# A fused two-layer network on one core: other rounds for the projections and the turns of tokens of the next image

## The chip, the cores and the metric

The kernel runs on one core of one Trainium2 chip. The metric is the device time of one execution in microseconds (us), the median of several executions. The engines are named as the profile names them: PE (TensorE, matmuls; PEld its weight loads), DVE (VectorE), ACT (ScalarE), POOL (GpSimd) and SP (SyncE, which issues DMAs). PE writes its results into PSUM, a small memory of eight banks per partition, from which ACT and DVE read.

## What is computed

Two layers on an input of 8 images of 128 channels and 32 x 32 pixels. The change lies in the first step of layer 0, attention along the rows of an image. Cut to what matters:

```python
def _L0_conv_ref(x, wq, wk, wv):
    xp = jnp.transpose(x, (0, 2, 3, 1))
    q = (xp @ wq.T).reshape(b, h, w, n, d)      # n = 8 heads, d = 16
    k = (xp @ wk.T).reshape(b, h, w, n, d)
    v = (xp @ wv.T).reshape(b, h, w, n, d)
    weights = jnp.einsum('bhwnd,bxynd->bnhwxy', q, k) * scale
    weights = jax.nn.softmax(weights, axis=-1)   # over y alone
    attn = jnp.einsum('bnhwxy,bxynd->bhwnd', weights, v)
    return jnp.transpose(attn.reshape(b, h, w, c), (0, 3, 1, 2))
...
x = x + _L0_conv_ref(_ln_c(x), L0_conv_wq, L0_conv_wk, L0_conv_wv)
t = t + _L0_ffn_ref(_ln_t(t), ...)      # a spectral filter of the tokens
x = x + _L1_conv_ref(_ln_c(x), ...)     # a deformable convolution
t = t + _L1_ffn_ref(_ln_t(t), ...)      # a mixture of eight experts
```

Every one of the 1024 tokens of an image looks at all 1024, but the softmax is taken over each group of 32 tokens by itself. `_ln_c` normalises each pixel over its channels.

## The kernel before

Attention comes first and takes about a third of the span; the other three steps follow, and the change does not touch them. The inputs of this case take the function `attention_bounded`. It works in *rounds*. An image has 8 units (4 quarters of 256 queries, `qc`, times 2 groups of 4 heads, `hg`), and a unit has 4 rounds, so an image has 32 rounds and the whole 256. Image b starts at round `first = 32 * b`. In the text, "round 20" means round 20 of the 32 of whichever image is running, and "-8" means `first - 8`, which is round 24 of the image before.

The function writes a list `work` of pieces, each with a round and an order within the round, sorts it, and issues it in that order; no scheduler changes it afterwards. Each engine runs its own instructions in this order and waits in it. For a unit that starts in round t0 the pieces are:

- order 0, round t0 + r: `scores`, 8 matmuls on PE into the PSUM tile `s` (four banks, one buffer; L609), then the exponential of all of it on ACT (L614), into `e`.
- order 1, the same round: `add_tiles` on POOL (L623).
- order 2, rounds t0 + 8 to t0 + 11: `values` on PE (L661), 8 calls a round in the first, third and fourth, with 4 more of the next piece at order 6.5 in the first and the last 4 of it in the second.
- order 2.5, round t0 + 6: `spread_out` on PE (L644).
- order 3, rounds t0 + 6 to t0 + 9: `divide` on DVE (L651).
- orders 4 and 5, round t0 + 5: `sums` on PE (L630, 16 matmul calls), then `reciprocals` on DVE (L637).
- for every second unit, order 5, round t0 + 11: `take` on ACT (L671); order 6, round t0 + 12: `results`, 2 matmuls `po` on PE (L678), a copy `at<-po` on ACT (L682), an addition on POOL (L686), and after the last quarter the DMA of the image to `x1d` (L688). `results` thus always falls on a round that is 0 mod 8.

As every t0 is a multiple of 4, a round's work depends on its number mod 4: sums are in 1 mod 4, `spread_out` in 2 mod 4, one and a half pieces of `values` in 0 mod 4, and 3 mod 4 has only scores and one piece of `values` on PE. (The profile counts each fp32 matmul call as two instructions.)

Between these lie the preparations of the next image:

- `load` (order 6): one DMA on SP's queue into `xc`.
- `tokens` (order 5.5), twice: four transposes on PE (`pt`, L544) and a copy on ACT (`xt<-pt`, L546). `xt` has three buffers.
- the layer norm in 25 small pieces (order 6): 8 of statistics on DVE (L77, L78), 9 on POOL, 8 on ACT (L103), which write `ht`.
- `channels` (order 5.5), twice: four transposes on PE (`pb`, L552) and a copy on ACT (`hk<-pb`, L555).
- ten projections (order 6): `keys` (L578, copy L583), `queries` (L564, L569) and `key_values` (L590, L596), each one or four matmuls on PE with 512 columns in all and a copy of 512 columns on ACT.

`po`, `pt`, `pb`, `pk`, `pq`, `pv` and the sums `z` all come from `small_bank` (L532), one PSUM bank under the tag "z", in a pool with one buffer (L521). A piece that takes it waits until the reader of the piece before has read it. Pieces with the same round and order go in the order in which they were put on the list, the images one after the other, so `results` of an earlier image or quarter that fall into the same round as a projection of the next image stand before it. `project_at`, `turn` and `norm_at` (L710 to L722) hold the rounds of the preparations.

Of the kernel before, what the change touches and what calls it, by code (L numbers as in the profile page):

```python
# [63 lines left out]
def layer_norm_pieces(nc, pool, src, dst, eps):  # L64

    t = {}

    def stats(i):  # L70
        if i == 0:
            for name, shape in (
                ("st", [P, NT, 6]), ("mv", [P, NT, 2]), ("v", [P, NT]), ("y", [P, NT]),
                ("w", [P, NT]), ("nm", [P, NT]),
            ):
                t[name] = pool.tile(shape, F32, tag=f"lp_{name}", name=f"lp_{name}")
        nc.vector.bn_stats(t["st"][:, i, :], src()[:, i, :])  # L77
        nc.vector.bn_aggr(t["mv"][:, i, :], t["st"][:, i, :])  # L78

    def inverse(n):  # L80

        v, y, w, mv = t["v"], t["y"], t["w"], t["mv"]
        bits = [i.bitcast(I32) for i in (y, v)]
        ops = [
            lambda: nc.gpsimd.tensor_scalar(v, mv[:, :, 1], eps, None, ALU.add),
            lambda: nc.gpsimd.tensor_scalar(bits[0], bits[1], -0.5, 0x5F3759DF, ALU.mult, ALU.add),
            lambda: nc.gpsimd.tensor_scalar(v, v, -0.5, None, ALU.mult),
        ]
        ops += 3 * [
            lambda: nc.gpsimd.tensor_mul(w, y, y),  # L90
            lambda: nc.gpsimd.tensor_mul(w, w, v),
            lambda: nc.gpsimd.tensor_scalar(w, w, 1.5, None, ALU.add),
            lambda: nc.gpsimd.tensor_mul(y, y, w),
        ]
        ops += [
            lambda: nc.gpsimd.tensor_mul(t["nm"], mv[:, :, 0], y),
            lambda: nc.gpsimd.tensor_scalar(t["nm"], t["nm"], -1.0, None, ALU.mult),
        ]
        for op in ops[2 * n : 2 * n + 2]:
            op()  # L100

    def norm(i):
        nc.scalar.activation(  # L103
            dst()[:, i, :], src()[:, i, :], AF.Identity, bias=t["nm"][:, i : i + 1],
            scale=t["y"][:, i : i + 1],
        )

    return (
        [partial(stats, i) for i in range(NT)] + [partial(inverse, n) for n in range(9)]
        + [partial(norm, i) for i in range(NT)]  # L110
    )
# [388 lines left out]
def attention_bounded(ctx, tc, ident, x, x1d, given, weigh, begin_group):  # L500
# [192 lines left out]
    def at(round_no, order, do, *args):  # L693
        work.append((round_no, order, len(work), do, args))

    def spread_rounds(pieces, rounds):
        for piece, round_no in zip(pieces, rounds):
            at(round_no, 6, piece)

    for b in range(B):  # L700
        img = {}
        first = 4 * UNITS * b
        project = [
            (keys, img, 0, 0), (keys, img, 0, 1), (queries, img, 0, 0),
            (keys, img, 1, 0), (keys, img, 1, 1), (queries, img, 1, 0),
            (key_values, b, img, 0), (key_values, b, img, 1),
            (queries, img, 0, 1), (queries, img, 1, 1),
        ]
        if b == 0:
            turn = {"tokens": (0, 0)}  # L710
            project_at = (-1, -1, -1, 0, 1, 2, 3, 4, 7, 11)
        else:
            project_at = [first + n for n in (-13, -12, -9, -5, -4, -1, 3, 4, 7, 11)]
            turn = {"channels": (first - 20, first - 17)}
            if b == 1:
                turn.update(load=0, tokens=(2, 3))
                norm_at = (3, 3, 4, 4, 5, 5, 6, 6) + (6, 7, 7, 8, 8, 8, 9, 9, 9) + (
                    10, 10, 10, 11, 13, 13, 14, 14)
            else:
                turn.update(load=first - 42, tokens=(first - 38, first - 34))  # L720
                norm_at = [first - n for n in (
                    37, 36, 35, 34, 33, 32, 32, 31, *range(31, 22, -1), 22, 22, 22, 21, 19, 19, 18, 18  # L722
                )]
        if b:
            at(turn["load"], 6, load, b)
            spread_rounds(
                layer_norm_pieces(nc, sb, lambda i=img: i["xt"], lambda: given.ht, 1e-6), norm_at
            )
            for par in range(2):
                at(turn["channels"][par], 5.5, channels, par)  # L730
        for par in range(2):
            at(turn["tokens"][par], 5.5, tokens, img, par)
        for n, (step, when) in enumerate(zip(project, project_at)):
            if b == 0 and n < 3:
                at(-1, 6, weigh[n])
            at(when, 6, *step)
        for qc in range(QC):
            qrt = {}
            for hg in range(HG):
                un = {"at": (qc, hg)}  # L740
                t0 = first + 4 * (HG * qc + hg)
                for r in range(4):
                    at(t0 + r, 0, scores, img, un, r)
                    at(t0 + r, 1, add_tiles, un, r)
                    at(t0 + 5, 4, sums, un, r)
                    at(t0 + 6 + r, 3, divide, un, r)
                at(t0 + 8, 2, values, img, un, 0, (0, 1), qrt)
                at(t0 + 8, 6.5, values, img, un, 1, (0,), qrt)
                at(t0 + 9, 2, values, img, un, 1, (1,), qrt)
                at(t0 + 10, 2, values, img, un, 2, (0, 1), qrt)  # L750
                at(t0 + 11, 2, values, img, un, 3, (0, 1), qrt)
                at(t0 + 5, 5, reciprocals, un)
                at(t0 + 6, 2.5, spread_out, un)
            at(t0 + 11, 5, take, qrt)
            at(t0 + 12, 6, results, b, img, qc, qrt)
# [889 lines left out]
def metaformer_kernel(  # L1645
# [27 lines left out]
    with tc.If(bounded > P - 1) as branch:  # L1673
        with ExitStack() as part:
            attention_bounded(part, tc, ident, x, x1d, given, weigh, begin.pieces)
# [63 lines left out]
```

## Time and profile before

| | |
|---|---|
| median of 3 runs | 2681.59 us (2681.54 to 2681.8) |
| profiled execution, its time | 2682.64 us |
| its span, first to last instruction | 2680.9 us |
| first to last exponential of attention | 30.1 to 889.3 us |
| PE busy in the span | 2518.2 us (94%) |
| DVE, POOL, ACT busy in the span | 1857.6, 1448.4, 1074.7 us |
| granted TensorE clock, mean of the span; of 100 to 850 us | 0.972; 1.00 |
| one exponential (L614) | 1879 ns, x256 |
| one divide (L651), one addition (L623) | 2278 ns, 2376 ns, x256 each |
| copies on ACT of 512 columns (L546, L555, L569, L583, L596) | median 586 to 603 ns |
| copies on ACT of 256 columns (L671, L682) | median 365, 366 ns |

A line of a group reads: source line, engine, operation, tiles written and read, shapes, count, then busy time and mean time of one, then the idle time of the engine just before it and what ended that idle time. Modelled ends of pipelined matmuls overlap a little, so a group that follows another on PE starts some 0.07 us before the other's shown end. A line of the timeline reads: start, duration, engine, source line, operation, tiles, shapes, count, and in brackets the engine's idle time before it with what ended it.

### The profile page before, as it was taken

The page shows a single profiled execution, that of the slowest core. Times are in us where ns is not written, and L with a number is a line of the kernel's source. Part 1 is how long each engine was busy: PE and PEld are TensorE (multiplying, and loading weights), DVE is VectorE, ACT ScalarE, POOL GpSimd, SP SyncE. Part 2 cuts the span into 40 slices and gives each one's busy share as a digit, 9 for nine tenths or more (in the row PEclk, how much of TensorE's full clock was granted, in tenths as well). Part 3 has the DMA queues.
Part 4 walks back from the last instruction along what each step waited for, and adds up shares of the span by engine and source line. Part 5 has one row for each costly group of instructions (what it writes and reads, how often), then busy time and mean ns, then how long its engine had stood idle before and what let it go on. Part 6 is the DMA issues. An engine that isn't in the chain of part 4 may idle for free. (4 is left out here: it accounts for less than half of the span.)

```text
span 2680.9 us, 47231 instructions
## 1 busy us (share of the span) xinstructions
PE 2518.2 (94%) x18768; PEld 1758.2 (66%) x18768; DVE 1857.6 (69%) x2744; ACT 1074.7 (40%) x2014; POOL 1448.4 (54%) x1535
## 2 busy tenths in 40 slices
PE   6999999999999799999999999999999999999914
PEld 3555555555555478787777778778778778778712
DVE  3788888888888545548748738748748657758646
ACT  4676766766667211123223224214224224224222
POOL 4777777777788455446246236236237327226230
PEclk9999999999999899999999999999999999999956
DMA  1000000000000254475266265256266256246151
GB/s 29 2 17 2 17 17 2 17 2 18 10 18 17 63 172 150 133 209 177 71 203 189 72 196 176 89 179 194 79 185 187 92 161 209 87 138 217 46 171 34
DMA packets 213379, 271.29 MB, mean 101 GB/s; under 512 B 20820, under 2 KB 146964, under 8 KB 213152
## 3 DMA queue, kind: packets, MB, share of 16 engines
q1 hardware_dynamic: 190016, 209.46, 26.1%
q0 software_dynamic: 16800, 55.59, 6.3%
q10 hardware_dynamic: 6336, 3.15, 0.4%
q8 instruction: 150, 2.46, 0.4%
q14 instruction: 77, 0.63, 0.1%
HBM read 200.22 MB, written 67.92 MB: 100 GB/s over the span
## 5 line engine op out<-in xcount | busy, mean ns | idle before, releaser
L623 POOL TENSOR_TENSOR t<-e 128x1024 f32<-128x1024 f32 x256 | 608.2, 2376 | 200.9 <-ACT e L614 200.6
L651 DVE TENSOR_TENSOR e<-e,rb 128x2048 f32<-128x2048 f32 x256 | 570.8, 2278 | 83.6 <-PE rb L644 83.6
L614 ACT ACTIVATE e<-s 128x2048 f32<-128x2048 f32 x256 | 481.1, 1879 | 253.8 <-PE s L609 251.8
L1508 POOL TENSOR_TENSOR part<-us,part 128x256 f32<-128x256 f32 x256 | 189.8, 742 | 695.5 <-ACT part L1507 694.9
L1460 PE MATMUL po<-us,mf 128*128 128x128 f32 (+2 forms) x2048 | 529.0, 381 | 4.4 <-DVE mf L1392 4.4
L1513 DVE TENSOR_TENSOR part<-p_y,part 128x512 f32<-128x512 f32 x256 | 175.5, 686 | 303.7 <-PE p_y L1495 177.0
L1506 ACT COPY us<-p_x 128x256 f32<-128x256 f32 x256 | 95.0, 371 | 724.2 <-PE p_x L1495 721.9
L1460 PEld LDWEIGHTS po<-us,mf 128*128 128x128 f32 x2048 | 309.2, 191 | 36.4 <-DVE mf L1392 4.8
L609 PE MATMUL s<-q,k 32*128 32x256 f32 x4096 | 296.9, 404 | 14.3 <-ACT e L614 13.5
L661 PE MATMUL av<-e,vt 128*32 128x256 f32 x4096 | 288.7, 389 | 4.4 <-DVE e L651 3.1
L1523 DVE TENSOR_TENSOR us<-p_z,part 128x512 f32<-128x512 f32 x256 | 174.9, 683 | 150.7 <-PE p_z L1495 150.6
L609 PEld LDWEIGHTS s<-q,k 32*128 32x128 f32 x4096 | 186.7, 186 | 137.3 <-ACT e L614 116.0
L1495 PEld LDWEIGHTS p_z<-diff,gap 128*128 128x128 f32 x1024 | 192.2, 190 | 128.0 <-issue 87.9
L1495 PE MATMUL p_z<-diff,gap 128*128 128x256 f32 x1024 | 264.8, 380 | 3.5 <-DVE base L906 3.1
L1107 ACT ACTIVATE g<-g,w 128x128 f32<-128x128 f32 x512 | 161.4, 394 | 112.2 <-DMA g<-tab,here 90.8
L1089 POOL DMA_INDIRECT g<-tab,here x168 | 166.0, 988 | 69.7 <-issue 30.5
L661 PEld LDWEIGHTS av<-e,vt 128*32 128x32 f32 x4096 | 101.4, 109 | 141.8 <-issue 84.5
L1115 DVE TENSOR_REDUCE x<-g 128x128 f32<-128x1536 f32 x64 | 180.4, 2818 | 6.8 <-ACT g L1107 1.2
L1250 POOL TENSOR_TENSOR diff<-teto 128x516 f32<-128x516 f32 x127 | 163.9, 1291 | 1.3 <-DMA teto<-in_phi_o 0.5
L637 DVE RECIPROCAL r<-z 128x256 f32<-128x256 f32 x64 | 112.5, 1758 | 70.8 <-PE z L630 70.6
L1495 PE MATMUL p_y<-diff,gap 128*128 128x256 f32 x512 | 152.9, 380 | 0.1
L1495 PE MATMUL p_z<-teto,ht 128*128 128x256 f32 x512 | 133.0, 382 | 0.0
(262 smaller groups left out, 3702.6 us busy)
## 6 DMA issues: line engine op xcount, KB each, us to landing
mf<-mfd SPq DMA_DIRECT2D x112, 512.0 KB
tab<-gs SPq DMA_DIRECT2D x180, 256.0 KB
teto<-in_phi_o SPq DMA_DIRECT2D x127, 256.5 KB
teto<-in_phi_e SPq DMA_DIRECT2D x127, 256.0 KB
mfd<-mf SPq DMA_DIRECT2D x16, 512.0 KB
xc<-in_x SPq DMA_DIRECT2D x8, 512.0 KB
x1d<-xt SPq DMA_DIRECT2D x8, 512.0 KB
m_room<-in_M_plus SPq DMA_DIRECT2D x16, 256.0 KB
```

The source lines that it names most:

```text
L609: nc.tensor.matmul(s[:, j, c, :], img["k"][rows, hg, 2 * r + c, :], q[rows, qc * QU : (qc + 1) * QU], start=True, stop=True,)
L614: nc.scalar.activation(e.rearrange("p j c q -> p (j c q)"), s.rearrange("p j c q -> p (j c q)"), AF.Exp, scale=float(HD) ** -0.5,)
L623: nc.gpsimd.tensor_add(t, e[:, :, 0, :], e[:, :, 1, :])
L651: nc.vector.tensor_tensor(e, e, un["rb"].unsqueeze(2).to_broadcast([P, NH, 2, QU]), ALU.mult)
L661: nc.tensor.matmul(qrt["av"][32 * j : 32 * j + 32, 0:QU], img["v"][:, 2 * r + c, P * hg + 32 * j : P * hg + 32 * j + 32], un["e", r][:, j, ...
L1089: nc.gpsimd.indirect_dma_start(out=tiles[-1][:, tap].rearrange("p k c -> p (k c)"), out_offset=None, in_=rows, in_offset=bass.IndirectOffs ...
L1115: nc.vector.tensor_reduce(x3[:, i, :], g.rearrange("p t k c -> p c (t k)"), AX.X, ALU.add)
L1460: self.nc.tensor.matmul(out, lhsT, rhs, start=bank not in img["opened"], stop=last, skip_group_check=True)
L1495: nc.tensor.matmul(out, weights, moving, start=start, stop=stop, skip_group_check=True)
L1508: nc.gpsimd.tensor_add(part[:, 0], mine[:, :, 0:P], part[:, 1])
L1513: nc.vector.tensor_tensor(part[:, 2:4], y[:, 0].unsqueeze(1).to_broadcast([C, 2, 2, P]), part[:, 0:2], ALU.add)
L1523: nc.vector.tensor_tensor(result(2, 4), z, part[:, 2:4], ALU.add)
```

## The change

Only lists of rounds are changed, for images 1 to 7; image 0's own lists stay as they are.

```diff
             (key_values, b, img, 0), (key_values, b, img, 1),
-            (queries, img, 0, 1), (queries, img, 1, 1),
+            (queries, img, 1, 1), (queries, img, 0, 1),
         ]
...
         else:
-            project_at = [first + n for n in (-13, -12, -9, -5, -4, -1, 3, 4, 7, 11)]
-            turn = {"channels": (first - 20, first - 17)}
+            project_at = [first + n for n in (-17, -13, -9, -8, -5, -1, 3, 7, 8, 11)]
+            turn = {"channels": (first - 20, first - 16)}
...
-                turn.update(load=first - 42, tokens=(first - 38, first - 34))
+                turn.update(load=first - 48, tokens=(first - 44, first - 36))
                 norm_at = [first - n for n in (
-                    37, 36, 35, 34, 33, 32, 32, 31, *range(31, 22, -1), 22, 22, 22, 21, 19, 19, 18, 18
+                    42, 41, 40, 39, 34, 33, 32, 31, *range(31, 22, -1), 22, 22, 22, 21, 19, 19, 18, 18
                 )]
```

By round of the 32, for a steady image in the middle (the next image's preparations and its own late projections):

| piece | round before | round after |
|---|---|---|
| keys (0,0), keys (0,1) | 19, 20 | 15, 19 |
| queries (0,0) | 23 | 23 |
| keys (1,0), keys (1,1) | 27, 28 | 24, 27 |
| queries (1,0) | 31 | 31 |
| key_values 0, key_values 1 | 3, 4 | 3, 7 |
| queries (0,1) | 7 | 11 |
| queries (1,1) | 11 | 8 |
| channels 0, channels 1 | 12, 15 | 12, 16 |
| tokens 0, tokens 1 (images 2 to 7) | 26, 30 | 20, 28 |
| load (images 2 to 7) | 22 | 16 |
| first four pieces of statistics (images 2 to 7) | 27, 28, 29, 30 | 22, 23, 24, 25 |
| last four of them | 31, 0, 0, 1 | 30, 31, 0, 1 |

No instruction is added or removed.

## The prediction

> **What bounds the kernel now.** I read the windows of the span first. From 100 to 800 us, in attention, PE is busy over 99% of each 100 us at full clock, with DVE at 82 to 84, POOL at 76 to 80 and ACT at 67 to 69. That modelled 99% hides small waits, so I read the list of waits (100 to 840 us, 'who line <- releaser line: us, times, longest') and the page's group of the exponential:
>
> ```profile
> L614 ACT ACTIVATE e<-s 128x2048 f32<-128x2048 f32 x256 | 481.1, 1879 | 253.8 <-PE s L609 251.8
> ...
> ACT e L614 <- PE s L609: 217.8, 215, 1.5
> ...
> PEld s L609 <- ACT e L614: 93.4, 186, 1.5
> ...
> DVE e L651 <- PE rb L644: 73.3, 56, 1.8
> ```
>
> ACT waits for the scores, PE waits for the exponential: a ring of two, because tile s has one buffer. Every round must run exp (1.88 us), then scores, then the next exp. In the timeline, scores start 1.24 us before the exp that reads them (442.24 to 443.48 below). A round whose other work on PE fits under exp takes about 1.88 + 1.24 plus a hand-over: the starts 437.02 and 440.21 give 3.19, 420.46 and 423.60 give 3.14. I take 3.17 as a free round. So only one question counts per round: when can PE begin the next scores?
>
> I then took the start of each of the 256 exps from the timeline (the first is round 0) and subtracted neighbours. Rounds 1 mod 4 cost 3.4 (16 matmuls of sums). Beyond that, by round mod 32: rounds 0, 8, 16, 24 (results) 3.28 to 3.31, and five dear ones: 4 (3.73), 20 (3.71), 28 (3.70), 26 (3.81), 30 (3.82). The five are where the old lists put projections at 0 mod 4 (-12, -4, 4) and tokens at 2 mod 4 (-38, -34). Projections at 3 mod 4, and channels, cost nothing above 0.07. Image 7, with nothing in rounds 20 and 28, shows 3.17 and 3.15 there.
>
> Timeline (start us, us, engine line op names): a projection in round 20 of image 3, then results in its round 24:
>
> ```profile
> 426.77 1.88 ACT L614 ACTIVATE e<-s 128x2048 f32<-128x2048 f32 x1 [0.56 <-PE s L609]
> 427.61 1.13 PE L578 MATMUL pk<-hk,diff 128*128 128x512 f32 x2
> 428.67 0.64 PE L661 MATMUL av<-e,vt 128*32 128x256 f32 x8
> 429.24 1.15 PE L609 MATMUL s<-q,k 32*128 32x256 f32 x16
> 430.48 1.88 ACT L614 ACTIVATE e<-s 128x2048 f32<-128x2048 f32 x1 [1.11 <-PE s L609]
> ...
> 440.21 1.88 ACT L614 ACTIVATE e<-s 128x2048 f32<-128x2048 f32 x1 [0.57 <-PE s L609]
> 441.03 0.71 PE L678 MATMUL po<-pick,o 128*128 128x128 f32 x4
> 441.67 0.64 PE L661 MATMUL av<-e,vt 128*32 128x256 f32 x8
> 441.99 0.36 ACT L682 COPY at<-po 128x256 f32<-128x256 f32 x1
> 442.24 1.15 PE L609 MATMUL s<-q,k 32*128 32x256 f32 x16
> 443.48 1.88 ACT L614 ACTIVATE e<-s 128x2048 f32<-128x2048 f32 x1 [1.12 <-PE s L609]
> ```
>
> Write E for the round's exp start. PE is through with whole values at E+0.82. The keys add 1.06 net (the next op starts at 428.67), po 0.64, the half of values 0.57. Scores thus start at E+2.47 with keys, at E+2.03 with po, against an exp that ended at E+1.88. Note also the copy: ACT is in order, so at<-po cannot run before E+1.78, though po was there at E+1.53.
>
> **The change part by part.** *Gains.* Old round 4 of images 1 to 7 becomes free: 7 x (3.73 - 3.17) = 3.9. Tokens leave rounds 26 and 30 of images 0 to 5: 6 x (0.64 + 0.65) = 7.7. Rounds 20 and 28 lose their keys in images 0 to 6 and get tokens in 0 to 5. Four token transposes take 0.74 (448.75 in the timeline), as long as po's 0.71, so such a round should be like a results round, 3.30: 6 x (0.41 + 0.40) + 2 x 0.53 = 5.9. Gains: 17.5 us.
>
> *Cost.* Three steps now land on 0 mod 8, where results are: channels(1) at -16, keys(1,0) at -8, queries(1,1) at +8. All of them, and po, take the same one-buffer PSUM tile (tag "z"). In the built order PE's queue reads there: whole values, pb, po, half values, scores (round 16), and whole values, po, pk or pq, half values, scores (rounds 24 and 8). The second user must wait until ACT has copied the first out, and that copy stands behind the running exp. Queued behind the wait on PE are half of the values and the next scores, and behind these the next exp, which is the ring itself. Nothing covers it. The startup rounds show such a hand-over:
>
> ```profile
> 41.55 0.74 PE L544 MATMUL pt<-ident,xc 128*128 128x128 f32 x4
> 41.72 1.88 ACT L614 ACTIVATE e<-s 128x2048 f32<-128x2048 f32 x1 [0.81 <-PE s L609]
> 43.49 0.58 ACT L546 COPY xt<-pt 128x512 f32<-128x512 f32 x1
> 44.12 1.13 PE L564 MATMUL pq<-hk,diff 128*128 128x512 f32 x2 [1.83 <-ACT xt L546]
> ```
>
> The copy begins at E+1.77, and pq 0.05 after its end. So, for rounds 24 and 8: at's copy ends at E+1.78+0.36 = 2.14; pk starts at 2.19, half values at 3.25, scores at 3.82, next exp at 5.06. Against 3.29: +1.77, 14 times, 24.8 us. Round 16: hk's copy (0.58 in round 12, at 82.81) ends at 2.36; po at 2.41, half values at 3.05, scores at 3.62, exp at 4.86; against 3.28: +1.58, 7 times, 11.1 us. Cost: 35.9 us.
>
> This exact sequence at full clock is nowhere in the trace, so I bound it. Below: the hand-over free, PE's own time alone, E+0.82+0.64+1.06+0.57+1.24 = 4.33 (+1.04), and 0.79+0.59+0.64+0.57+1.24 = 3.83 for round 16 (+0.55): 18.4 us. Above: the startup round itself took 5.38 (41.72 to 47.10), +2.1 each: 44.1 us. I take 35.9, summed from full-clock rows of the same operations; the startup round had its scores at half clock (1.87 instead of 1.15).
>
> *Moved at no cost.* Projections among the rounds 3 mod 4 (15, 19, 23, 27, 31, 3, 7, 11): covered by exp as before (3.19 with one, 3.17 free); uncovered, 1.06 each. ACT copies of 0.6 lie in ACT's wait for scores. Statistics move by 5 rounds (first half) and 0 or 1 (second): at most three pairs of 0.47 now precede one reciprocal, where there were up to four; DVE idles about 1.3 before the divides (73.3 / 56) and 0.9 before the reciprocal (51.2 over 56 units) in each unit. Were that gone, 0.47 each would delay reciprocal, spread and scores. The load moves past nothing on SP: in both orders it follows the x1d write of the image three before, and is issued right behind it (499.45 and 499.89); DMA in 500 to 600 us is done in two or three slices of 2.5 us. So tokens, 12 rounds after that write instead of 18, wait neither for xc nor for xt. POOL's queue keeps its order.
>
> *Sum.* +35.9 - 17.5 = +18.4. The profiled span, 2680.9, becomes 2699.3; the median of the runs shown is 0.7 above that span, so **2700 us**. What follows attention depends on its end and moves with it.
>
> **The clock.** The granted clock fell after startup: stretches of 3.41 us (us, PE busy, PEld, DVE, ACT, POOL, PEclk, DMA share, GB/s):
>
> ```profile
> 42.04:45.45 3.41, 1.58 (x9) 0.63 (x11) 1.25 (x7) 2.19 (x3) 2.60 (x2) 1.00 0.02 5
> 45.45:48.87 3.42, 2.66 (x20) 1.51 (x16) 0.31 (x2) 2.19 (x2) 0.57 (x1) 0.50 0.00 0
> 59.11:62.52 3.41, 2.52 (x33) 1.63 (x31) 2.80 (x6) 1.88 (x1) 2.52 (x2) 1.00 0.02 5
> 62.52:65.94 3.42, 2.45 (x30) 1.22 (x22) 3.35 (x6) 2.35 (x2) 2.70 (x4) 1.00 0.01 2
> ```
>
> 1.58 busy was followed by half clock, 2.52 and 2.45 were not; elsewhere 1.95 was (at 2090.04), 2.25 was not (at 1267.43). A collision idles PE for 0.66 (E+1.53 to 2.19) or 0.96 (1.45 to 2.41), leaving at least 2.4 of 3.41. So by the rows the clock stays; there is little to spare.
> The Trainium skill, "TensorE: Matmul & The Clock Gate", section "A second HAM failure mode: psum-queue depth-cycling", speaks against the change: cycling through PSUM banks with short PE idles between groups made the clock swing there. By the page's halved clock, the sum would be that of the first rival; the rows above are nearer, and I keep to them.
>
> **The rivals.** (1) *Half clock after collisions* (0.08): idle as above takes a 3.41 us stretch below the limit between 1.95 and 2.25. Each then loses up to half, 1.7 us: 7 of them give 2712, all 21 give 2736. For: the startup. Against: 2.4 busy is above what kept its clock.
> (2) *The hand-over is hidden* (0.06), only PE's own time counts: +18.4 - 17.5 = +0.9, 2682.5. For: PE's weight loads run ahead of its matmuls in many rows. Against: the 1.83 us wait for xt above.
> (3) *Faster* (0.05): the wait for at's copy takes in the keys' time, so that a results round with a projection costs what a projection alone does, 3.71, and pb beside po is free: 14 x 0.42 = 5.9 against 17.5, 2670. It decides from a mean price per collision below 17.5 / 21 = 0.83. For: 3.71 was measured in rounds 20 and 28. Against: it needs copies before E+1.78, and none in the timeline is.
> (4) That "3 mod 4" is not what is done is true in part: -8 and 8 are 0 mod 8; without them and -16 only the gains would stand, 2664. The built order puts them beside results in all 21 rounds.
>
> **How the numbers follow.** The forecast has 0.81. Its own range, 2693 to 2707, takes the collision at 1.4 to 2.05 each with the gains kept (21 x 1.4 - 17.5 = +11.9, 21 x 2.05 - 17.5 = +25.6). The range, 2689 to 2712, adds a collision of 1.2 (halfway to a free hand-over) below and the cheap end of rival 1 above; rivals 2, 3 and the rest of 1 stay outside. A measurement of this kernel tells 0.2%, 5.4 us, from no change. Faster: rival 3, 0.05. Same: rival 2, 0.06. Slower: forecast and rival 1, 0.89.
>
> **What would show it.** From exp to exp: rounds 8 and 24 at 5.06, 16 at 4.86, 20 and 28 at 3.30, 26, 30 and 4 at 3.17; waits of po on hk L555 (7) and of pk and pq on at L682 (14), 0.7 to 1.0 each; granted clock 1.00 from 100 to 850 us. Wrong if these rounds stay below 4.1 (rival 2 or 3), if the clock falls, or if DVE's reciprocals start to hold back spread.

## The result, and the profile after

The changed kernel takes 2702.0 us (median of 4 runs, 2701.0 to 2705.9), against 2681.7 for the kernel before (4 runs of it, 2681.5 to 2688.1): a ratio of 1.007, 95% interval 1.0052 to 1.0088. It is slower by about 20 us. The profiled execution has a span of 2700.9 us, 20.0 more than before.

The prediction counts in exponentials (exps): the first is round 0, and each round lasts from its exp's start to the next one's. Taken from the timeline of each kernel and worked out by subtraction:

```
                              before     after   difference
start to exp 0                 30.1       30.0      -0.2
exp 0 to exp 8                 36.2       34.4      -1.9    (startup)
exp 8 to exp 255              821.0      840.0     +19.0    (forecast +18.4)
last exp to the end          1793.5     1796.6      +3.1
rounds, all images together:
  8: +12.3    16: +11.0    24: +12.4                         = +35.8
  4:  -3.9    20:  -2.9    26:  -3.8    28: -2.8   30: -3.8  = -17.3
  all others from exp 8 on: +0.4
  2 and 3 of image 0 (startup): -1.8
```

The first new form is a collision in round 24 of image 3, in the timeline (start us, us, engine line operation tiles shapes count, in brackets the idle time before and what ended it):

```profile
447.09 1.88 ACT L614 ACTIVATE e<-s 128x2048 f32<-128x2048 f32 x1 [0.56 <-PE s L609]
447.90 0.71 PE L678 MATMUL po<-pick,o 128*128 128x128 f32 x4
448.87 0.37 ACT L682 COPY at<-po 128x256 f32<-128x256 f32 x1
449.28 1.12 PE L578 MATMUL pk<-hk,diff 128*128 128x512 f32 x2 [0.67 <-ACT at L682]
450.34 0.64 PE L661 MATMUL av<-e,vt 128*32 128x256 f32 x8
450.91 1.15 PE L609 MATMUL s<-q,k 32*128 32x256 f32 x16
452.15 1.88 ACT L614 ACTIVATE e<-s 128x2048 f32<-128x2048 f32 x1 [1.11 <-PE s L609]
```

Read it from the exp's start at 447.09 (E, as in the prediction). The matmuls po end at 448.61, but ACT is still in the exp, so the copy of po begins at 448.87 (E+1.78). PE stands until 449.28 with the keys, and behind the keys wait the half of values and the next scores. The next exp starts at E+5.06; in the kernel before, this round took 3.27. Round 16 has the same form with the transposes of channels as first user:

```profile
419.51 1.88 ACT L614 ACTIVATE e<-s 128x2048 f32<-128x2048 f32 x1 [0.54 <-PE s L609]
420.35 0.66 PE L552 MATMUL pb<-ident,ht 128*128 128x128 f32 x4
421.29 0.58 ACT L555 COPY hk<-pb 128x512 f32<-128x512 f32 x1
421.92 0.71 PE L678 MATMUL po<-pick,o 128*128 128x128 f32 x4 [0.91 <-ACT hk L555]
423.13 1.15 PE L609 MATMUL s<-q,k 32*128 32x256 f32 x16
424.35 1.88 ACT L614 ACTIVATE e<-s 128x2048 f32<-128x2048 f32 x1 [1.25 <-PE s L609]
```

A gain looks like this: round 26 of image 3, first in the kernel before, where the transposes of tokens (448.75) lie between the exp and the next one, then in the changed kernel, where they are gone and the next exp starts after 3.14 us instead of 3.76:

```profile
446.90 1.88 ACT L614 ACTIVATE e<-s 128x2048 f32<-128x2048 f32 x1 [1.54 <-PE s L609]
...
448.75 0.74 PE L544 MATMUL pt<-ident,xc 128*128 128x128 f32 x4
...
450.66 1.88 ACT L614 ACTIVATE e<-s 128x2048 f32<-128x2048 f32 x1 [0.55 <-PE s L609]
```

```profile
455.57 1.88 ACT L614 ACTIVATE e<-s 128x2048 f32<-128x2048 f32 x1 [1.54 <-PE s L609]
...
458.71 1.88 ACT L614 ACTIVATE e<-s 128x2048 f32<-128x2048 f32 x1 [1.27 <-PE s L609]
```

On the page the exponential's group shows ACT's idle time, 253.8 us before:

```profile
L614 ACT ACTIVATE e<-s 128x2048 f32<-128x2048 f32 x256 | 481.1, 1879 | 262.7 <-PE s L609 260.6
```

That is only 9 us more: part of ACT's longer idle time now stands before the copies of the collisions instead, so this line alone would mislead. In the list of waits (100 to 860 us; total, times, longest) the new entries stand by name, below the ring's own two:

```profile
ACT e L614 <- PE s L609: 228.2, 217, 1.6
...
PEld s L609 <- ACT e L614: 99.7, 194, 1.5
...
PE po L678 <- ACT hk L555: 5.4, 6, 1.0
...
PE pk L578 <- ACT at L682: 4.6, 7, 0.7
PE pq L564 <- ACT at L682: 4.5, 7, 0.7
```

PE waits 14.5 us there in all, and none of these three existed before. That is less than half of the +35.8. The rest is near the 18.4 that the prediction gave for PE's own work without any wait: the second user's matmuls (about 1.06 us for keys or queries, 0.64 for po) do not fit under the exponential beside the rest of the round. So the price of a collision is about half wait and half work. The clock did not fall. Stretches of 3.41 us (us, then busy time of PE, PEld, DVE, ACT, POOL, the granted clock, DMA share, GB/s), the first with the collision of round 16 above in it, the last the least busy one with a collision:

```profile
418.63:422.04 3.41, 2.50 (x37) 1.33 (x30) 3.41 (x3) 2.70 (x3) 2.62 (x2) 1.00 0.00 0
422.04:425.45 3.41, 3.41 (x52) 2.09 (x56) 2.03 (x1) 1.48 (x2) 2.56 (x2) 1.00 0.00 0
637.08:640.49 3.41, 2.45 (x34) 1.28 (x30) 3.41 (x3) 2.54 (x3) 2.58 (x2) 1.00 0.00 0
```

### The profile page after: what moved, and what is told of

Same layout as the page of the kernel before. It is cut to its first block, busy times and chain, and to the rows that moved or that the text cites. A ratio compares the mean times of both kernels' runs of the same rounds, so it can differ in the third digit from the quotient of the medians.

```text
span 2700.9 us, 47216 instructions
## 1 busy us (share of the span) xinstructions
PE 2515.0 (93%) x18768; PEld 1755.8 (65%) x18768; DVE 1855.7 (69%) x2744; ACT 1072.9 (40%) x2014; POOL 1447.4 (54%) x1535
## 3 DMA queue, kind: packets, MB, share of 16 engines
q10 hardware_dynamic: 6336, 3.15, 0.4%
```

## The experiments

**The gap filled.** In the colliding rounds the half of values is put between the two users of the bank.

```diff
-            at(when, 6, *step)
+            at(when, 6.5, *step)
...
-                at(t0 + 8, 6.5, values, img, un, 1, (0,), qrt)
+                at(t0 + 8, 6.1, values, img, un, 1, (0,), qrt)
...
-            at(t0 + 12, 6, results, b, img, qc, qrt)
+            at(t0 + 12, 6.2 if qc == 0 and b + 1 < B else 6, results, b, img, qc, qrt)
```

> The changed kernel, with the half of values that stood behind the second user of the bank put before it in the 21 colliding rounds; no work is added or removed. Theory (PE waits for the copy of the first user): the half values run inside that wait, so each collision gets 0.57 us cheaper: rounds 8 and 24 from 5.06 to 4.49, round 16 from 4.86 to 4.29, together 21 x 0.57 = 12.0 us less than the changed kernel, about 2690. Rival (the rounds are dear because they hold more PE work than fits under the exponential): the same work in another order, so no change, about 2702.

Measured: rounds 8 and 24 at 4.49 to 4.54, round 16 at 4.26 to 4.34, each of the 21 collisions 0.57 us cheaper; from exp 8 to exp 255, 828.1 us, 11.9 less than the changed kernel. Round 24 of image 3:

```profile
443.32 0.71 PE L678 MATMUL po<-pick,o 128*128 128x128 f32 x4
443.96 0.64 PE L661 MATMUL av<-e,vt 128*32 128x256 f32 x8
444.28 0.37 ACT L682 COPY at<-po 128x256 f32<-128x256 f32 x1
444.70 1.12 PE L578 MATMUL pk<-hk,diff 128*128 128x512 f32 x2
445.75 1.15 PE L609 MATMUL s<-q,k 32*128 32x256 f32 x16
```

The wait of 0.67 is down to 0.10 (from 443.96 + 0.64 = 444.60 to 444.70), because the half of values now runs inside it. The same work in another order is cheaper, so the wait itself was being paid for, and the rival of work alone falls as the whole cause. The total says it less sharply: 2695.3 (10 runs) beside 2684.4 for the kernel before on that chip (29 runs), ratio 1.0037 (1.0024 to 1.005), +10.9 where the theory with the changed kernel's 2702 would have +8.3. The 2690 expected was missed by 5 us, of which 2.7 is that the kernel before itself was slower there. The changed kernel was not run beside these; the +8.3 lies inside the interval, which in us is +6.4 to +13.4.

**One collision alone**, in the kernel before:

```diff
-            turn = {"channels": (first - 20, first - 17)}
+            turn = {"channels": (first - 20, first - 16)}
```

> The kernel before, with channels(1) at -16 instead of -17 and nothing else. Theory: round 16 of images 0 to 6 goes from 3.28 to 4.86 and nothing is gained, 7 x 1.58 = +11.1 us on before, about 2693. Rival (only PE's own time counts): round 16 at 3.83, 7 x 0.55 = +3.9, about 2686. Rival (the dear rounds come from the whole new rhythm, not from one step): round 16 stays near 3.3.

Measured: round 16 goes to 4.83 to 4.91, +11.06 over the seven images; no other round outside the startup changes by more than noise. Exp 8 to exp 255 takes 832.0, +10.9; the median is 2695.2 against 2684.4, ratio 1.0038 (1.0025 to 1.005). One step moved by one round costs 11 us, with the rest of the rhythm as it was. The price of PE's own work alone would have been 3.9.

**Tokens back** to rounds 26 and 30, in the changed kernel:

```diff
-                turn.update(load=first - 48, tokens=(first - 44, first - 36))
+                turn.update(load=first - 42, tokens=(first - 38, first - 34))
                 norm_at = [first - n for n in (
-                    42, 41, 40, 39, 34, 33, 32, 31, ...
+                    37, 36, 35, 34, 33, 32, 32, 31, ...
```

> The changed kernel with tokens, load and statistics of images 2 to 7 back at their old rounds (tokens at -38 and -34); the projections and channels stay as changed. Theory: rounds 26 and 30 go back to 3.81 (+0.64 and +0.65), rounds 20 and 28 fall from 3.30 to 3.17, 6 x (0.64 + 0.65 - 0.13 - 0.13) = +6.2 us on the changed kernel, about 2708: this part of the change is a gain by itself. Rival (where tokens are put does not count, they are hidden): no change, about 2702.

Measured: round 26 +3.7, round 30 +3.9, round 20 -0.8, round 28 -1.0 over the six images; exp 8 to exp 255 takes 845.6, +5.6 on the changed kernel (forecast +6.2). The median is 2710.1, ratio to before 1.0094 (1.0073 to 1.0114), 25.7 us over before where the changed kernel had 20.3. So the move of tokens is a gain of its own, within a change that loses.

**Without results.** The body of `results` is left away except for the DMA.

```diff
     def results(b, img, qc, qrt):
-        if qc == 0:
-            img["at"] = sb.tile([P, NT, C], F32, tag="at", name="at", bufs=1)
-        po = small_bank("po")
...
-        nc.gpsimd.tensor_add(mine[0], mine[0], mine[1])
         if qc == QC - 1:
             nc.sync.dma_start(x1d[b], img["xt"])
```

> The changed kernel without the matmuls, the copy and the addition of results: x1 is then the turned input without the attention's output, and everything else runs as it did. So nothing shares a round with pb, pk or pq any more. Theory (a collision is po's own time plus the wait for its copy): rounds 24 and 8 fall from 5.06 to the 3.71 of a projection alone in a 0 mod 4 round (1.35 less, of which 0.64 is po's own work and 0.7 the wait), round 16 from 4.86 to 3.24, round 0 from 3.3 to 3.17. Rival (these rounds are dear for another reason: the projections in 0 mod 8, or the divides that hold back values): they stay above 4.3, which is 5.06 less po's own work.

Measured: rounds 24 and 8 at 3.65 to 3.75, round 16 at 3.23, round 0 at 3.14 to 3.22. Round 24 of image 3:

```profile
433.05 1.88 ACT L614 ACTIVATE e<-s 128x2048 f32<-128x2048 f32 x1 [0.59 <-PE s L609]
433.83 1.12 PE L578 MATMUL pk<-hk,diff 128*128 128x512 f32 x2
434.89 0.64 PE L661 MATMUL av<-e,vt 128*32 128x256 f32 x8
435.46 1.15 PE L609 MATMUL s<-q,k 32*128 32x256 f32 x16
```

The keys start at E+0.78 instead of E+2.19. With one user of the bank the round costs just what a projection in a 0 mod 4 round cost before; the number 0 mod 8 has nothing to it. This kernel also lacks the addition on POOL that belongs to `results`; the gap filled, which keeps every instruction, shows that the wait is the cause without this doubt. Its one timed run was 2665.0, too few to compare totals.

**No collision at all.** A list of our own, from the kernel before, with only transposes in the rounds 20 and 28 and one projection in a round 2 mod 4:

```diff
-            project_at = [first + n for n in (-13, -12, -9, -5, -4, -1, 3, 4, 7, 11)]
-            turn = {"channels": (first - 20, first - 17)}
+            project_at = [first + n for n in (-17, -13, -9, -5, -1, 3, 4, 7, 10, 11)]
+            turn = {"channels": (first - 20, first - 12)}
...
-                turn.update(load=first - 42, tokens=(first - 38, first - 34))
+                turn.update(load=first - 42, tokens=(first - 36, first - 34))
...
-                    37, 36, 35, 34, 33, 32, 32, 31, ...
+                    35, 35, 35, 34, 33, 32, 32, 31, ...
```

(The order of the steps in `project` is changed to suit, and image 0 keeps its own.)

> From the kernel before: channels(1) at -12 (round 20), first tokens at -36 (round 28), the ten projections at -17, -13, -9, -5, -1, 3, 4, 7, 10, 11, so that nothing of the next image shares a round with results and only one projection lies in a round 2 mod 4 (10). Theory (transposes fit into 0 mod 4, a projection in 2 mod 4 costs its 1.06 on PE because spread fills that round): round 20 from 3.71 to 3.24, round 28 to 3.30, round 26 to 3.17, round 10 from 3.17 to 4.23; 7 x (1.06 - 0.47) - 6 x (0.40 + 0.64) - 0.53 = -2.6 us on before, about 2679. Rival (reciprocals, which hold the bank, end later than it seems, so a projection in 2 mod 4 waits as in a collision): round 10 near 5, +3 us or more on before.

Measured: rounds 20 (3.21 to 3.26), 26 (3.14 to 3.22) and 28 (3.30 to 3.34) came as expected, but round 10 took 4.69 to 4.74 in images 1 to 6 instead of 4.23, and round 3, of which nothing was expected, 3.83 to 3.93 instead of 3.18. Exp 8 to exp 255: 826.1, +5.1 on before; median 2691.0 (12 runs) where 2679 was expected, ratio 1.0025 (1.0013 to 1.0037). A miss, with the rival's number and not its cause. First round 3, then round 10 of an image:

```profile
477.88 0.59 ACT L569 COPY q<-pq 128x512 f32<-128x512 f32 x1
478.52 1.15 PE L609 MATMUL s<-q,k 32*128 32x256 f32 x16 [0.68 <-ACT q L569]
...
501.76 1.13 PE L564 MATMUL pq<-hk,diff 128*128 128x512 f32 x2
502.82 1.15 PE L609 MATMUL s<-q,k 32*128 32x256 f32 x16
502.93 0.59 ACT L569 COPY q<-pq 128x512 f32<-128x512 f32 x1 [1.19 <-PE pq L564]
503.41 1.26 ACT L103 ACTIVATE ht<-xt,lp_nm,lp_y 128x128 f32<-128x128 f32 x3
504.57 1.86 ACT L614 ACTIVATE e<-s 128x2048 f32<-128x2048 f32 x1
```

In round 3 the scores wait for the copy of queries(1,0), which they read at once: the step had been put one round before its reader. In round 10 PE did begin the scores at 502.82, on time, without any wait for the bank. But ACT, late with the copy, then had three steps of the layer norm (1.26 us) in front of the next exp. Image 7 supports this: in its round 10 only one such step stands there, and the round took the 4.22 expected:

```profile
824.84 0.50 ACT L103 ACTIVATE xc<-xc,lp_nm,lp_y 128x128 f32<-128x128 f32 x1
...
825.49 1.88 ACT L614 ACTIVATE e<-s 128x2048 f32<-128x2048 f32 x1 [0.15 <-PE s L609]
```

**No collision, on time.** Two changes in that list follow: queries(1,0) and keys(1,1) are exchanged, to -1 and 3, and queries(1,1) goes from 10 to 6, where ACT has no layer norm.

> As the run without collisions, with two steps of its list exchanged so that no reader waits: queries(1,0) at -1 and keys(1,1) at 3, since queries(1,0) at 3 were read by the next scores and round 3 took 3.88; and the projection in a 2 mod 4 round at 6 instead of 10, where three steps of the layer norm stood on ACT behind its copy and round 10 took 4.71. Theory: round 3 back to 3.18, round 10 to 3.17, round 6 at 4.2; attention 0.45 us an image or about 3 us shorter than before, apart from the startup, about 0.1%, which the total hardly tells. Rival (a projection in a 2 mod 4 round costs 1.5 wherever it stands): round 6 at 4.7, attention no shorter than before.

Measured: round 3 is back at 3.15 to 3.22, round 10 at 3.14 to 3.19, and round 6 takes 4.14 to 4.25. Exp 8 to exp 255 takes 818.2, 2.85 less than before and 21.8 less than the changed kernel. In total 2684.4 (12 runs) against 2685.8 (17), ratio 0.9995 (0.9986 to 1.0005): attention is shorter in the profile, the whole kernel is not told from the one before.

## Why the prediction was right, by its steps

- *What bounds attention*: the ring of exp and scores. In every run, from exp 12 on, each exp started 1.21 to 1.29 us after its scores did, so the round was set by when PE could begin them. The one exception is round 10 of the run without collisions, at 1.75 to 1.76, where ACT was late.
- *The collisions*: 5.06 and 4.86 a round were forecast, 5.06 to 5.11 and 4.83 to 4.91 measured, 35.8 us in all against 35.9. The cause, the wait for the first user's copy with half values and scores behind it, is shown by the gap filled (the wait is what gets cheaper: it was 15.4 us in all 21 collisions, and 11.9 were saved) and by leaving out results (without the first user, or the second, no collision).
- *The gains*: 17.3 against 17.5. Rounds 20 and 28 came at 3.27 to 3.35 instead of 3.30, rounds 4, 26 and 30 at 3.17 on average, as forecast. That the gain in rounds 26 and 30 belongs to tokens was shown by putting tokens back. Round 4 kept a projection in the last two experiments, and stayed at 3.66 to 3.79 there.
- *Nothing from the steps moved at no cost*: the rounds 15, 19, 23, 27, 31, 3, 7 and 11 are as before within noise, and no wait for xc or xt appeared. Nor did reciprocals hold back spread more than before: PE's weight loads for it waited 23.8 us for reciprocals or statistics (100 to 860 us), against 23.9.
- *Rival 1, half clock*: no stretch of half clock between 53.4 and 923.8 us. The least busy stretch of this part with a collision had 2.45 of 3.41 busy. That is above every stretch at full clock that half clock followed in these traces; the busiest of those had 2.12 (2493.28:2496.69 in the run with the gap filled). But the limit that the prediction put between 1.95 and 2.25 is not there: in the kernel before, 76.17:79.58 had only 1.92 and the next stretch ran at full clock, and in the changed kernel so did the one after 910.14:913.56, with 1.69. So the forecast that the clock stays was right, while PE's busy time in one stretch does not by itself say when it falls. What does was not tested. The Trainium skill's warning ("TensorE: Matmul & The Clock Gate", "A second HAM failure mode: psum-queue depth-cycling") did not come true here at PE idles of 0.62 to 0.96 us, three times in 32 rounds.
- *Rivals 2 and 3*: both needed the wait to be hidden; the timeline shows it in 21 rounds, a collision cost 1.70 on average (35.8 / 21) where rival 3 needed less than 0.83, and the collision alone cost 11.06 against rival 2's 3.9.
- *The range*: its low end took a collision of 1.2 us as halfway to a free hand-over. Halfway between the prediction's own 1.71 (35.9 / 21) and 0.88 (18.4 / 21) is 1.29, so the low end should have been 2691 by its own rule. Nothing else hangs on it.

What the sum did not have is the +1.6 between its 18.4 and the span's 20.0. Of this, 0.6 lies between exp 8 and exp 255; the rest is two differences that the sum had left out and that nearly cancel, which is luck. Up to exp 8, 2.1 was gained, most of it in two rounds: rounds 2 and 3 of image 0 vary with where a half-clock stretch falls (10.2 us of it before, 3.4 after, none in two of the experiments, where rounds 2 and 3 took 4.67 and 4.73 instead of 5.38 and 6.59). And the part after the last exp took 3.1 more. Its code is the same in all kernels. It took 1796.6 to 1798.5 in the five experiments with full attention, with either rhythm, so nothing shows that it belongs to the change; why the one profile of before has 1793.5 was not settled. Half clock after 880 us does not explain it: 142.4 us before, 137.4 after.

## What to carry to other kernels

A round's number in a hand-written rhythm stands for what else lies there. Before moving a step, list who uses the same single PSUM buffer in the target round: two users in one round cost the copy of the first, and if the copying engine runs in order behind a long instruction, the wait lasts until that instruction ends, with all that is queued behind it exposed. If two users must share a round, put independent matmuls between them: here this saved 0.57 us of 1.70 on average each time. And a step's deadline is its copy's end, not its own round.

## What the runs showed of the hardware

- A copy on ACT starts about 0.1 us before the exponential in front of it ends (448.87, with the exp at 447.09 + 1.88 = 448.97), and PE starts some 0.05 us after a copy that it waited for. Both held in all 21 collisions, to 0.01 us.
- PE's granted clock stayed full in the changed kernel from 53.4 to 923.8 us, where collisions left PE idle for up to 0.96 us at a time. Busy time in one stretch of 3.41 us at full clock did not decide what came next: after 1.69 us (changed kernel, 910.14) and 1.92 (before, 76.17) the clock stayed full, after 1.95 (before, 2090.04) and 2.12 (the gap filled, 2493.28) it was halved.
- The same part of the program, after attention, differed by up to 5 us between the profiled executions of the seven kernels that keep `results` (1793.5 to 1798.5), more than the 2.9 us that the best list gained.
